# Even steps in a new order, and the keys' transpose moved to PSUM bank Y

## Chip, core and metric

The kernel runs on one core of one Trainium2 chip. The metric is the device time of one execution in microseconds (us). It is given as the median of several runs; a separate profiled execution has a time of its own, and its trace is where durations in this document come from.

## What is computed

An attention layer with 16 query heads and one shared pair of key and value heads, over 64 entries of 128 tokens with 512 features, in float32. For each entry:

```
xn  = layernorm(x, g_in)                       # 128 x 512
q   = xn @ Wq  -> 16 heads of 64, times 64**-0.5
k,v = xn @ Wkv -> 64 + 64, with one null key and value in front
sim = q k^T + attn_bias   (masked: causal, and the entry's padding)
out = softmax(sim) v      -> 128 x 1024
x   = x + layernorm(out @ Wo, g_out)
```

## The kernel before

The program is one long list of instructions whose order is written by hand: `manual_schedule()` keeps each engine's instructions in the order in which the Python code emits them. The tile framework adds semaphores wherever one instruction needs another's result or a buffer that another still uses. An engine works through its list in order, so an instruction that waits holds up all that stand behind it on its engine.

After a prologue, a loop calls `step(n)` for n = -6 to 62. One step works on several entries at once, each at another stage. Numbers below are for step n in the steady part of the loop:

- the queries of four entries (a group) are made over four steps, with seven products of half size in place of eight (`product(g, f, 1..7)`, line 436, names `pa`, `pc`, `pw`). Each product is four instructions on TensorE. Their results are read from PSUM by ScalarE (`keep`, names `ku`, `kp`, line 447; `q_out` without a name, line 454) or by VectorE (`q_out` with a name, line 457, `qT<-pc,ku` and `qT<-pw,kp`).
- the scores of entry n+2: `scores(b, 0)` and `scores(b, 1)` (line 500, `ps`) for lower and upper tokens. Both use the same PSUM buffer `s`, so the second half waits until VectorE has taken the first one out (`scores_add`, line 513). `scores_max` (line 518) finds the negated row maximum of each half.
- the softmax of entry n+1: `exps` on ScalarE (line 527, one instruction for each head row), `rinv` on VectorE (line 544), `scale` on GpSimd (line 548), `blocks_T` on VectorE (line 580, `sb`), and 14 DMAs (`blocks_move`, line 606) which put the transposed blocks into `aTb`.
- the values of entry n: `values` and `values_end` (line 641, `po`), taken out by ScalarE (line 685, `oT`). A one-element copy `done` (line 673) on VectorE stands between the two.
- keys and values of later entries: `k_T` (line 356) transposes the keys of entry n+5 and `kv_mm` (line 321) multiplies for entry n+6, both into one PSUM tile `pk`. VectorE reads `pk` three times: `kT_out` (line 361), and `kv_out` (lines 335 and 344).
- the output product, done for two entries together with seven products (`out_product`, line 755, names `pyX`, `pyY`, `pyw`, eight instructions each). Products 1, 2 and 4 stand in even steps, the others in odd steps. `out_part` (line 778) and `out_keep` (lines 767, 769) take results out.
- the output norm of the two entries of a pair, in even steps: `pair_stats`, `pair_pow` (GpSimd), `pair_nmr` (line 799, `nmro`, a tiny VectorE instruction), `pair_norm` (line 809, ScalarE writes `yn` into PSUM bank Y), `pair_residual` (VectorE: line 813 multiplies by `gob` in place in bank Y, line 814 adds the residual into `y`), then `store`.

All eight PSUM banks are in use: two for `s`, one each for `a`, `c`, `X`, `Y`, and two in turn for tag `w`. In the kernel before, `pk` is a `w` tile. Bank Y holds in turn `yn` of the first entry and `yn` of the second entry (even step), then `pyY` (odd step).

The instructions of a step that the prediction follows, in the order of the code for an even step: product 4 of the pair, first `exps`, `pair_stats`, `rinv(eb, 0)`, output product 1, query product 2, `pair_norm(p4)` and its residual, output product 2 (`pyw`), more `exps`, query product 1, the rest of `exps`, `rinv(eb, 1)`, `scale`, `pair_norm(p4 + 1)`, query product 5, `scores(nb, 0)`, `scores_add(nb, 0)`, `values`, `pair_residual(p4 + 1)`, `blocks_T`, `scores_max(nb, 0)`, `scores(nb, 1)`, `scores_add(nb, 1)`, `values_end`, query product 6, `k_T` and `kv_mm`, query product 7, `q_out(..., "c", "u3")`, `scores_max(nb, 1)`, `kT_out`, `kv_out`. In odd steps `scores_max(nb, 1)` comes ahead of product 6. The next step begins with query product 2 (odd steps), then query products 4 and 3; product 3 adds onto the bank `c` which `q_out(..., "c", "u3")` reads.

Of the kernel before, what the change touches and what calls it, by code (L numbers as in the profile page):

```python
# [8 lines left out]
FP = mybir.dt.float32  # L9
U8 = mybir.dt.uint8  # L10
AF = mybir.ActivationFunctionType
ALU = mybir.AluOpType
# [5 lines left out]
def kernel(  # L18
# [59 lines left out]
    nc = tc.nc  # L78
    B, N, DIM = x.shape
    H = attn_bias.shape[0]  # L80
    DH = w_kv.shape[1] // 2
    P = 128
# [3 lines left out]
    GB = 4  # L86
    NG = B // GB
    TOK = GB * N
    KVN = 2 * DH
# [22 lines left out]
    xs, res, m8s = {}, {}, {}  # L112
# [141 lines left out]
    def norm_stats(m):  # L254
        st = small.tile([P, 6], FP, tag="st", name=f"st_{m}")
        nc.vector.bn_stats(st, xs[m])
        mv = small.tile([P, 2], FP, tag="mv", name=f"mv_{m}")
        nc.vector.bn_aggr(mv, st)
        rstd = small.tile([P, 1], FP, tag="rstd", name=f"rstd_{m}")
        nc.vector.tensor_scalar(rstd, mv[:, 1:2], EPS, None, ALU.add)  # L260
        nc.gpsimd.tensor_tensor(rstd, rstd, nhalf, ALU.pow)  # L261
        stats[m] = mv, rstd
# [53 lines left out]
    def kv_mm(m, pkv=None):  # L316
        g, t = divmod(m, GB)
        if pkv is None:
            pkv = ps_w.tile([P, KVN], FP, tag="w", name=f"pkv_{m}")
        for kc in range(KC):  # L320
            nc.tensor.matmul(  # L321
                pkv,
                xT[g][:, t, kc, :],
                wkv[:, kc, :],
                start=(kc == 0),
                stop=(kc == KC - 1),
            )
        return pkv
# [3 lines left out]
    def kv_out(m, pkv):  # L332
        g, t = divmod(m, GB)
        k = bp.tile([P, 2, DH], FP, tag="ktok", name=f"ktok_{m}")
        nc.vector.tensor_tensor(
            k,
            pkv[:, 0:DH].unsqueeze(1).broadcast_to([P, 2, DH]),
            nkv[:, 0:DH].unsqueeze(1).broadcast_to([P, 2, DH]),
            ALU.subtract,
        )  # L340
        ktok[m] = k
        if t == 0:
            vs[g] = hp.tile([P, GB, DH], FP, tag="vs", name=f"vs_{g}", bufs=3)
        nc.vector.tensor_tensor(vs[g][:, t, :], pkv[:, DH:], nkv[:, DH:], ALU.subtract)
# [8 lines left out]
    def k_T(m, pk=None):  # L353
        if pk is None:
            pk = ps_w.tile([P, N], FP, tag="w", name=f"pkT_{m}")
        nc.tensor.transpose(pk, ktok.pop(m).rearrange("p r d -> p (r d)"), ident)
        return pk

    def kT_out(m, pk):
        kT[m] = hp.tile([P, N], FP, tag="kT", name=f"kT_{m}", bufs=6)  # L360
        nc.vector.tensor_copy(kT[m], pk)
# [83 lines left out]
    def keep(tag, name):  # L445
        kept[name] = bp.tile([P, HT], FP, tag=f"k{name}", name=f"k{name}", bufs=1)
        nc.scalar.copy(kept[name], prod[tag])  # L447
# [63 lines left out]
    def scores_add(b, hf):  # L511
        sv = S[b][:, :, KEYS[hf]].rearrange("p (r f) j -> p r f j", r=2)
        nc.vector.tensor_tensor(sv, pss.pop((b, hf)), sv, ALU.add)  # L513

    def scores_max(b, hf):
        if hf == 0:
            nmax[b] = small.tile([P, 2, R8], FP, tag="nmax", name=f"nmax_{b}")
        nc.vector.tensor_reduce(  # L518
            nmax[b][:, hf], S[b][:, :, WITH_NULL[hf]], AX.X, ALU.max, negate=True
        )  # L520

    def exps(b, hf, lo=0, hi=R8):
        if hf == 0 and lo == 0:
            rsum[b] = small.tile([P, 2, R8], FP, tag="rsum", name=f"rsum_{b}")
        for k in range(lo, hi):
            row = S[b][:, k, WITH_NULL[hf]]
            nc.scalar.activation(  # L527
                row,
                row,
                AF.Exp,  # L530
                bias=nmax[b][:, hf, k : k + 1],
                accum_out=rsum[b][:, hf, k : k + 1],
            )
# [8 lines left out]
    def rinv(b, hf):  # L542
        rinvs[b, hf] = small.tile([P, R8], FP, tag="rinv", name=f"rinv_{b}_{hf}")
        nc.vector.reciprocal(rinvs[b, hf], rsum[b][:, hf])
# [149 lines left out]
    def out_mm(b, lo=0, hi=NC):  # L694
        if lo == 0:
            pool, tag = ps_w, "w"
            if b > P_LAST:
                pool, tag = (ps_q, "c") if b == P_LAST + 2 else (ps_y, "XY"[b % 2])
            py = pool.tile([P, DIM], FP, tag=tag, name=f"py_{b}")
            ys[b] = py  # L700
        for c in range(lo, hi):
            nc.tensor.matmul(  # L702
                ys[b],
                oT[b][:, c, :],
                wo[:, c, :],
                start=(c == 0),
                stop=(c == NC - 1),
            )
# [14 lines left out]
    def plain(b):  # L723
        return not (paired(b) or paired(b - 1))
# [39 lines left out]
    def out_keep(tag, name, slot):  # L764
        kept[name] = bp.tile([P, HE], FP, tag=f"k{slot}", name=f"k{name}", bufs=1)
        if name == "yu2":
            nc.vector.tensor_copy(kept[name], prod["y" + tag])  # L767
        else:
            nc.scalar.copy(kept[name], prod["y" + tag])
# [26 lines left out]
    def pair_nmr(b):  # L796
        mv, rstd = yn.pop(b)
        nmr = small.tile([P, 1], FP, tag="nmro", name=f"nmro_{b}")
        nc.vector.tensor_scalar(nmr, mv[:, 0:1], rstd, -1.0, ALU.mult, ALU.mult)  # L799
        nmrs[b] = nmr, rstd  # L800
# [9 lines left out]

    def pair_residual(b):
        z = yn.pop(b)
        nc.vector.tensor_tensor(z, z, gob, ALU.mult)
        nc.vector.tensor_tensor(ys[b], z, res.pop(b), ALU.add)

    def out_stats(b):
        st = small.tile([P, 6], FP, tag="st", name=f"sto_{b}")
# [44 lines left out]
    def step(n):  # L862
        def ok(b, end=B):
            return 0 <= b < end
# [11 lines left out]
        p12, p4, p5673 = n - 1, n - 3, n - 2  # L876
        first, third, second = paired(p12), paired(p4), paired(p5673)
        one = ok(n - 1) and plain(n - 1)
        def transfers():

            if n == 1:
                store(0)
            if n > B3 + 1 and ok(n - 2) and plain(n - 2):
                store(n - 2)
            loads_late(n)

        fill = n <= 0
        eb = n + 1 if n < B3 else n + 2  # L890
# [17 lines left out]
                token_sum(qg, k)  # L908
        for m in mns:
            norm_stats(m)  # L910
        if n == -4:
            bias_add(0)
            bias_add(1)
# [42 lines left out]
        if n == B3 - 1:  # L956
            scores(B3 + 1, 1)
            scores_add(B3 + 1, 1)
            scores_max(B3 + 1, 1)
        if third:  # L960
            pair_stats(p4 + 1)
        if 2 * GB <= mb < B:
            tokens_T(mb)
            if (mb + 1) % GB == 0:
                tokens_out(mb // GB)
        if soft and n != 1:
            exps(eb, 0, 4)
        if fast and f == 0 and not fill:
            token_sum(qg, 1)
        if soft and n not in (1, B3 + 1):  # L970
            rinv(eb, 0)
            scale(eb, 0)
        if third:
            pair_pow(p4 + 1)
# [29 lines left out]
        if n == B3:  # L1004
            out_keep("X", "yp1", "p1")
            scores(eb, 0)
            scores_add(eb, 0)
            scores_max(eb, 0)
            out_product(p12, 2, ps_w, "w")
            pair_norm(p4)  # L1010
            pair_residual(p4)
            store(p4)
            out_part(p12, 0, "w", "yp1")
            scores(eb, 1)
            scores_add(eb, 1)
            exps_half(eb, 0)
            scores_max(eb, 1)
        elif first:
            out_keep("X", "yp1", "p1")
            out_product(p12, 2, ps_w, "w")  # L1020
            out_part(p12, 0, "w", "yp1")
        if soft and n != 1:
            exps(eb, 1, 2, 4)
        if soft and not second:
            exps(eb, 1, 4, 6)
        if fast:
            product(qg, f, 1, ps_q, "a")
            keep("a", "p1")
            q_out(qg, f, lo_t, "w", "p1")
# [20 lines left out]
        if fast and f == 0 and not fill:  # L1050
            for k in range(3, 5):
                token_sum(qg, k)
        if fast:
            product(qg, f, 5, ps_q, "c")
        if second:
            out_product(p5673, 7, ps_y, "X", start=False)
# [9 lines left out]
        if n == B3 - 1:  # L1066
            exps_half(B3 + 1, 0)
            exps(B3 + 1, 1, 0, 3)
        if sc and n != B3:
            scores(nb, 0)  # L1070
            scores_add(nb, 0)
        split = sc and n != B3
# [30 lines left out]
            scores_max(nb, 0)  # L1103

        late = fast and (first or n < 0)
        if sc:
            scores(nb, 1)
            scores_add(nb, 1)
            if n == -1:
                rinv(0, 1)  # L1110
                scale(0, 1)
            if not late:
                scores_max(nb, 1)
        if ok(n) and split:
            values_end(n, split)
            if n > B3 + 1:
                out_mm(n - 1, NF)
        if one and n > 1:
            out_stats(n - 1)
        if eb == B - 1:  # L1120
# [20 lines left out]
            scale(B3 + 1, 1)  # L1141
        if n + 10 < 2 * GB:
            norm_T(n + 10)
        if ok(mkv) and mkv >= GB - 1:

            pk = ps_w.tile([P, KVN + N], FP, tag="w", name=f"pk_{mkv}")
            k_T(mk, pk[:, KVN:])
            kv_mm(mkv, pk[:, 0:KVN])


        if (n + 8) % GB == 0 and 2 <= (n + 8) // GB < NG:
            tokens_in((n + 8) // GB)
# [7 lines left out]
                scores_max(nb, 1)  # L1160
        if second:
            pair_stats(p5673)
        if ok(mkv) and mkv >= GB - 1:
            kT_out(mk, pk[:, KVN:])
            kv_out(mkv, pk[:, 0:KVN])
        if ok(mk) and not ok(mkv):
            kT_out(mk, k_T(mk))
        if n == B3 - 2:
# [111 lines left out]
```

## Time and profile before

| what | value |
|---|---|
| median of 3 runs | 1109.07 us (1108.53 to 1110.0) |
| the profiled execution's own time | 1106.42 us |
| its span, first to last instruction | 1104.5 us |
| mean granted TensorE clock | 0.997 |
| busy: PE / PE weight loads | 1081.3 us / 868.1 us |
| busy: DVE (VectorE) / ACT (ScalarE) / POOL (GpSimd) | 795.7 / 665.5 / 706.0 us |
| idle of ACT before `oT` (line 685), waiting for PE | 198.0 us |
| idle of PE weight loads before `ps` (line 500), waiting for DVE line 513 | 25.6 us, 61 times |

How to read it: busy time is the union of an engine's instructions in the profiled execution. PE is the matrix multiplication and PEld the load of its weights, which overlaps it. Matmuls are pipelined and their ends are modelled, so small waits of TensorE are seen best in the weight loads, whose starts are recorded. "A <- B" says that A sat idle until B was done.

### The profile page before, as it was taken

To read this page: it belongs to the slowest core of one execution; us is meant where nothing else is said; L and a number is where in the kernel's file an instruction comes from. 1 tells how busy PE (TensorE), PEld (TensorE's weight loads), DVE (VectorE), ACT (ScalarE), POOL (GpSimd) and SP (SyncE) were. 2 spreads that over 40 slices of the span, in tenths; PEclk is the share of its full clock that TensorE was granted. 3 is DMA by queue.
4 is the path that set the end of the run, shared out by engine and by line. 5 is a ranking of instruction groups with operands and counts; after the bars stand their busy time and mean duration, and the time that the engine had idled before them with its cause. 6 is when DMAs were issued, how large, how long until landed. Compare 5 with 4: busy or idle time off the path is not lost.

```text
span 1104.5 us, 27326 instructions
## 1 busy us (share of the span) xinstructions
PE 1081.3 (98%) x9794; PEld 868.1 (79%) x9794; DVE 795.7 (72%) x1729; ACT 665.5 (60%) x2645; POOL 706.0 (64%) x521
## 2 busy tenths in 40 slices
PE   8999999999999999999999999999999999999987
PEld 5576788888888888888888888888888888888643
DVE  4676677877867877776886777787777787666852
ACT  3265567666666656566756566766666665657651
POOL 2546958566676756767575675856667675676832
PEclk9999999999999999999999999999999999999999
DMA  6422354453534444353353435445353453422333
GB/s 198 129 76 62 81 150 112 134 131 89 159 99 139 125 128 122 91 167 107 121 138 113 126 101 149 115 131 132 87 159 99 134 130 116 113 63 76 97 106 100
DMA packets 101062, 129.81 MB, mean 118 GB/s; under 512 B 21312, under 2 KB 65728, under 8 KB 99136
## 3 DMA queue, kind: packets, MB, share of 16 engines
q1 hardware_dynamic: 99680, 126.70, 41.0%
q8 instruction: 78, 1.28, 0.5%
q10 hardware_dynamic: 1248, 1.38, 0.4%
q14 instruction: 56, 0.46, 0.1%
HBM read 54.86 MB, written 31.46 MB: 78 GB/s over the span
## 4 chain that ended last, share of the span: by engine, by line
PE 81%; DVE 5%; DMA 4%; ACT 4%; SPq 3%; POOL 2%; issue 1%; DVEq 0%; POOLq 0%; ACTq 0%
PE pa L436 17%; PE pyX L755 16%; PE pc L436 8%; PE pyY L755 8%; PE ps L500 8%; PE po L641 7%; PE pk L321 4%; PE pw L436 4%; PE pyw L755 4%; DMA x<-in_x_dram 3%; PE py L702 3%; ACT s L527 2%; SPq L606 2%; PE pq L387 1%; DVE s L513 1%
## 5 line engine op out<-in xcount | busy, mean ns | idle before, releaser
L527 ACT ACTIVATE s<-s,nmax 128x65 f32<-128x65 f32 (+1 forms) x1024 | 371.5, 367 | 0.0
L479 POOL TENSOR_TENSOR s<-biasp,mneg 128x1552 f32<-128x1552 f32 x64 | 205.3, 3208 | 112.0 <-DVE sb L580 108.8
L548 POOL TENSOR_TENSOR s<-s,rinv 128x512 f32<-128x512 f32 (+1 forms) x128 | 189.6, 1482 | 122.6 <-DVE nmro L799 89.1
L685 ACT ACTIVATE oT<-po,nv 128x512 f32<-128x512 f32 x128 | 81.0, 683 | 198.0 <-PE po L641 198.0
L527 ACT ACTIVATION_READ_ACCUMULATOR s<-s,nmax 128x1 f32 x1024 | 194.7, 190 | 0.0
L755 PE MATMUL pyX<-wT,oT 128*128 128x256 f32 x696 | 164.7, 379 | 0.5 <-DVE kyu L767 0.5
L755 PEld LDWEIGHTS pyX<-wT,oT 128*128 128x128 f32 x696 | 131.8, 190 | 19.6 <-DVE kyu L767 0.9
L500 PEld LDWEIGHTS ps<-kT,qT 64*64 64x64 f32 x4096 | 92.5, 134 | 48.1 <-DVE s L513 25.6
L513 DVE TENSOR_TENSOR s<-ps,s 128x512 f32<-128x512 f32 (+1 forms) x128 | 121.6, 950 | 10.1 <-PE ps L500 9.6
L436 PE MATMUL pa<-xS,wq 128*128 128x256 f32 x480 | 123.6, 380 | 1.0 <-ACT ku L447 1.0
L518 DVE TENSOR_REDUCE nmax<-s 128x8 f32<-128x520 f32 (+1 forms) x128 | 120.1, 938 | 1.3
L500 PE MATMUL ps<-kT,qT 64*64 64x64 f32 (+1 forms) x4096 | 116.7, 251 | 3.7 <-DVE done L673 2.0
L580 DVE STREAM_TRANSPOSE sb<-s 128x1536 f32<-128x1536 f32 x62 | 109.9, 1773 | 11.6 <-POOL s L548 4.3
L641 PE MATMUL po<-aTb,vs 64*64 64x256 f32 (+1 forms) x1240 | 115.3, 379 | 0.0
L436 PEld LDWEIGHTS pa<-xS,wq 128*128 128x128 f32 x480 | 86.2, 190 | 11.2 <-ACT ku L447 1.8
L447 ACT COPY ku<-pa 128x256 f32<-128x256 f32 x120 | 44.7, 373 | 82.5 <-PE pa L436 82.5
L261 POOL TENSOR_TENSOR rstd<-rstd,nhalf 128x1 f32<-128x1 f32 x64 | 35.7, 558 | 60.4 <-DVE rstd L260 55.4
L436 PE MATMUL pa<-xS,wS 128*128 128x256 f32 x240 | 67.8, 405 | 0.1
L809 ACT ACTIVATE yn<-y,nmro,rstdo 128x512 f32<-128x512 f32 x58 | 45.4, 782 | 36.2 <-DVE nmro L799 36.1
L321 PE MATMUL pk<-wkv,xT 128*128 128x128 f32 x488 | 64.5, 275 | 0.0
L457 DVE TENSOR_TENSOR qT<-pw,kp 128x256 f32<-128x256 f32 x60 | 25.4, 424 | 53.4 <-ACT kp L447 53.4
L641 PEld LDWEIGHTS po<-aTb,vs 64*64 64x64 f32 (+1 forms) x1240 | 55.8, 134 | 9.7 <-issue 4.1
(116 smaller groups left out, 2068.9 us busy)
## 6 DMA issues: line engine op xcount, KB each, us to landing
aTb<-sb SPq DMA_DIRECT2D x369, 64.0 KB
x<-in_x_dram SPq DMA_DIRECT2D x64, 256.0 KB
res<-in_x_dram SPq DMA_DIRECT2D x64, 256.0 KB
out_dram<-y SPq DMA_DIRECT2D x64, 256.0 KB
aTb<-sb SPq DMA_DIRECT2D x492, 32.0 KB
xd<-xb SPq DMA_DIRECT2D x14, 1024.0 KB
xT<-xd SPq DMA_DIRECT2D x56, 256.0 KB
wo<-in_L_cond_Wo_dram SPq DMA_DIRECT2D x1, 2048.0 KB
```

The costliest lines, as they stand in the source:

```text
L321: nc.tensor.matmul(pkv, xT[g][:, t, kc, :], wkv[:, kc, :], start=(kc == 0), stop=(kc == KC - 1),)
L436: nc.tensor.matmul(prod[tag], w[:, kc, f * P : (f + 1) * P], t[:, :, kc, :], start=(start and kc == 0), stop=(kc == HK - 1), skip_group_ch ...
L479: nc.gpsimd.tensor_tensor(S[b], biasp, mneg[:, t].unsqueeze(1).broadcast_to([P, R8, ROW]), ALU.add,)
L500: nc.tensor.matmul(pv[u * DH : (u + 1) * DH, r, f, :], qT[g][rows, f, t, hf, u], kT[b][rows, 0:nk], start=True, stop=True,)
L513: nc.vector.tensor_tensor(sv, pss.pop((b, hf)), sv, ALU.add)
L518: nc.vector.tensor_reduce(nmax[b][:, hf], S[b][:, :, WITH_NULL[hf]], AX.X, ALU.max, negate=True)
L527: nc.scalar.activation(row, row, AF.Exp, bias=nmax[b][:, hf, k : k + 1], accum_out=rsum[b][:, hf, k : k + 1],)
L548: nc.gpsimd.tensor_tensor(sv, sv, rinvs.pop((b, hf)).unsqueeze(2).broadcast_to([P, R8, sv.shape[2]]), ALU.mult,)
L580: nc.vector.transpose(sb.rearrange("p j e q -> p e j q"), S[b][:, :, 1 : ROW - 1].rearrange("p e (j k) -> p e j k", k=Q),)
L641: nc.tensor.matmul(pos[b][u][r * DH : (r + 1) * DH, half], vals[keys], aT_of(b)[keys, slots, r * NF : (r + 1) * NF], start=start, stop=Tru ...
L685: nc.scalar.activation(oT[b][:, u * NF : (u + 1) * NF, :].rearrange("p f (s q) -> p s f q", q=Q), po[u].rearrange("p h i f q -> p (h i) f q"),
L755: nc.tensor.matmul(prod[key], h[:, c, :], w[:, c, :], start=(start and c == 0), stop=(c == HC - 1), skip_group_check=not start,)
```

## The change

No instruction is added or taken away. The order changes, one PSUM tile moves to another bank, and one operand changes place:

- In even steps with a full set of work (n = 4, 6, ..., 56; `even` in the code) `pair_nmr` of the pair's first entry moves from inside `pair_norm` to just behind `norm_stats`; `rinv(eb, 0)` comes ahead of `pair_stats`; query product 1 with its `keep` and `q_out` comes ahead of output product 2; and query product 5, `scores(nb, 0)` and `scores_add(nb, 0)` come ahead of the last `exps`, `rinv(eb, 1)`, `scale` and `pair_norm` of the pair's second entry.
- `k_T` comes straight behind `values_end`, ahead of query product 6; `kv_mm` keeps its place behind product 6. Their tile `pk` is now in bank Y (from step 0 on).
- From step 3 on (`early`), `kT_out` and `kv_out` come straight behind `kv_mm`: in odd steps ahead of `scores_max(nb, 1)`, in even steps ahead of query product 7 and `q_out(..., "c", "u3")`.
- `pair_residual` writes the product with `gob` to `ys[b]` in SBUF in place of bank Y, and adds the residual there.

```diff
     def pair_residual(b):
         z = yn.pop(b)
-        nc.vector.tensor_tensor(z, z, gob, ALU.mult)
-        nc.vector.tensor_tensor(ys[b], z, res.pop(b), ALU.add)
+        nc.vector.tensor_tensor(ys[b], z, gob, ALU.mult)
+        nc.vector.tensor_tensor(ys[b], ys[b], res.pop(b), ALU.add)
...
+        even = first and third and fast
...
+        pks = []
+        if ok(mkv) and mkv >= GB - 1:
+            pks.append(None)
+
+        def keys_T(pool, tag):
+            pks[0] = pool.tile([P, KVN + N], FP, tag=tag, name=f"pk_{mkv}")
+            k_T(mk, pks[0][:, KVN:])
+
+        def keys_values_out():
+            kT_out(mk, pks[0][:, KVN:])
+            kv_out(mkv, pks[0][:, 0:KVN])
...
         for m in mns:
             norm_stats(m)
+        if even:
+            pair_nmr(p4)
...
+        if even:
+            exps(eb, 0, 4)
+            rinv(eb, 0)
         if third:
             pair_stats(p4 + 1)
...
+        elif even:
+            out_keep("X", "yp1", "u3")
+            product(qg, f, 1, ps_q, "a")
+            exps(eb, 1, 2, 4)
+            keep("a", "p1")
+            q_out(qg, f, lo_t, "w", "p1")
+            out_product(p12, 2, ps_w, "w")
+            out_part(p12, 0, "w", "yp1")
+            exps(eb, 1, 4, 6)
+            product(qg, f, 5, ps_q, "c")
+            scores(nb, 0)
+            scores_add(nb, 0)
         elif first:
             out_keep("X", "yp1", "p1")
             out_product(p12, 2, ps_w, "w")
             out_part(p12, 0, "w", "yp1")
...
         late = fast and (first or n < 0)
+        early = fast and n > 2 and pks
         if sc:
             scores(nb, 1)
             scores_add(nb, 1)
...
-            if not late:
+            if not late and not early:
                 scores_max(nb, 1)
...
+        if pks and ok(n):
+            keys_T(ps_y, "Y")
...
-        if ok(mkv) and mkv >= GB - 1:
-
-            pk = ps_w.tile([P, KVN + N], FP, tag="w", name=f"pk_{mkv}")
-            k_T(mk, pk[:, KVN:])
-            kv_mm(mkv, pk[:, 0:KVN])
-
+        if pks:
+            if not ok(n):
+                keys_T(ps_w, "w")
+            kv_mm(mkv, pks[0][:, 0:KVN])
+            if early:
+                keys_values_out()
+                if sc and not late:
+                    scores_max(nb, 1)
...
-        if ok(mkv) and mkv >= GB - 1:
-            kT_out(mk, pk[:, KVN:])
-            kv_out(mkv, pk[:, 0:KVN])
+        if pks and not early:
+            keys_values_out()
```

At their old places the moved lines are skipped in even steps (`and not even`).

More of the change, by code (lines that the diff above doesn't have):

```diff
@@ L965, in step @@
                 tokens_out(mb // GB)
-        if soft and n != 1:
+        if soft and n != 1 and not even:
             exps(eb, 0, 4)
@@ L970, in step @@
         if soft and n not in (1, B3 + 1):
-            rinv(eb, 0)
+            if not even:
+                rinv(eb, 0)
             scale(eb, 0)
@@ L1021, in step @@
             out_part(p12, 0, "w", "yp1")
-        if soft and n != 1:
+        if soft and n != 1 and not even:
             exps(eb, 1, 2, 4)
-        if soft and not second:
+        if soft and not second and not even:
             exps(eb, 1, 4, 6)
-        if fast:
+        if fast and not even:
             product(qg, f, 1, ps_q, "a")
@@ L1052, in step @@
                 token_sum(qg, k)
-        if fast:
+        if fast and not even:
             product(qg, f, 5, ps_q, "c")
@@ L1068, in step @@
             exps(B3 + 1, 1, 0, 3)
-        if sc and n != B3:
+        if sc and n != B3 and not even:
             scores(nb, 0)
```

## The prediction

> **What bounds the kernel now.** I read the page first (busy times), then the list of waits, then the timelines of the weight loads and of DVE over neighbouring steps in the middle of the run.
>
> ```profile
> PE 1081.3 (98%) x9794; PEld 868.1 (79%) x9794; DVE 795.7 (72%) x1729; ACT 665.5 (60%) x2645; POOL 706.0 (64%) x521
> ```
>
> ```profile
> PEld ps L500 <- DVE s L513: 25.6, 61, 1.7
> ```
>
> TensorE is the bound: DVE, ACT and POOL have more than a quarter of the span to spare, and its one repeated wait is the second half of the scores, on the add that empties their PSUM buffer. So an edit is worth what it does to TensorE's waits. I number times from T0, the first weight load of `ps` in a step. Step 24 (even, T0 = 472.38), loads:
>
> ```profile
> 472.38 0.56 PEld L500 LDWEIGHTS ps<-kT,qT 64*64 64x64 f32 x32 [0.33 <-issue]
> ...
> 473.89 0.86 PEld L500 LDWEIGHTS ps<-kT,qT 64*64 64x64 f32 x32 [0.25 <-DVE s L513]
> ...
> 475.36 0.73 PEld L436 LDWEIGHTS pa<-xS,wS 128*128 128x128 f32 x4 [0.39 <-issue]
> 476.24 0.14 PEld L356 LDWEIGHTS pk<-ident,ktok 128*128 128x128 f32 x1
> ...
> 479.71 0.84 PEld L436 LDWEIGHTS pc<-xT,wS 128*128 128x128 f32 x4
> ...
> 489.51 0.56 PEld L500 LDWEIGHTS ps<-kT,qT 64*64 64x64 f32 x32 [0.33 <-issue]
> ```
>
> and the same step on DVE:
>
> ```profile
> 473.14 0.69 DVE L513 TENSOR_TENSOR s<-ps,s 128x512 f32<-128x512 f32 x1
> ...
> 474.21 0.69 DVE L813 TENSOR_TENSOR yn<-yn,gob 128x512 f32<-128x512 f32 x1
> ...
> 477.81 1.21 DVE L513 TENSOR_TENSOR s<-ps,s 128x1024 f32<-128x1024 f32 x1
> ...
> 478.94 0.41 DVE L457 TENSOR_TENSOR qT<-pc,ku 128x256 f32<-128x256 f32 x1
> ...
> 480.40 0.28 DVE L361 COPY kT<-pk 128x128 f32<-128x128 f32 x1
> ```
>
> The scores and values take 2.98 us (472.38 to 475.36), and the next step's scores begin at T0 + 17.13. Step 26 (T0 = 504.91) is disturbed:
>
> ```profile
> 502.38 0.78 ACT L809 ACTIVATE yn<-y,nmro,rstdo 128x512 f32<-128x512 f32 x1 [1.80 <-DVE nmro L799]
> ...
> 506.22 0.20 DVE L544 RECIPROCAL rinv<-rsum 128x8 f32<-128x8 f32 x1 [0.35 <-ACT s L527]
> ...
> 506.54 0.68 DVE L513 TENSOR_TENSOR s<-ps,s 128x512 f32<-128x512 f32 x1
> ...
> 507.28 0.86 PEld L500 LDWEIGHTS ps<-kT,qT 64*64 64x64 f32 x32 [0.68 <-DVE s L513]
> ```
>
> ACT waited for `nmro`, so the exponentials ended late, DVE stood at `rinv`, and the add behind it came at T0 + 1.63 in place of 0.76. Reading T0 to the next T0 in the same timelines, the even steps 6, 10, 14, ... 54 exceed 17.13 by 0.06, 0.14, 0.49, 0.21, 0.38, 0.86, 0, 0.69, 1.03, 0.16, 0.67, 0 and 0 us: 4.7 us in all. Steps 4, 8, 12, ... are at 17.13 every time. Those 4.7 us are all that a smoother even step can bring.
>
> **The change part by part.** The work is the same, so only waits move.
>
> *nmro early, rinv early, scores ahead of the last exponentials.* `nmro` gets behind `rstd` (500.07 in step 26) and `yn` follows 0.20 later, as at 502.19 and 502.38; it may start at about 500.6, when ACT's two exponentials of the upper half are through. That takes 1.8 us from ACT's delay, so the exponentials end about 0.5 us before T0, and the add stands ahead of `rinv`: it starts at T0 + 0.76 always. Gain 4.7 us. Query product 1 and `pyw` change places, four and eight instructions back to back on TensorE: nothing; `y<-pyw` then has until the second `po` tile, over 0.9 us.
>
> *The keys' wait.* `pk` now takes bank Y, so the transpose waits until DVE has multiplied the second entry's `yn` by `gob`. `nmro` of that entry now stands behind the add. From T0: add 0.76; `rinv` 0.60 later (506.54 to the next start, 507.14), `nmro` 0.12 later (506.22 to 506.34), `yn` on ACT 0.20 later, the multiply 0.81 after that (502.38 to 503.19), which takes 0.69, and a load starts 0.06 after DVE's end (473.83 to 473.89): 0.76 + 0.60 + 0.12 + 0.20 + 0.81 + 0.69 + 0.06 = 3.24. TensorE is there at 2.98. A wait of 0.26 in every even step; before, product 6 stood there and waited for nothing of the kind, and the multiply began at 1.83. Queued behind the transpose on TensorE is everything else. On DVE, the multiply stands idle for `yn`, and the residual, `blocks_T`, maximum and second add stand behind it.
>
> *The second wait.* From the multiply's start to the second add's start DVE needs 3.60 (474.21 to 477.81), so the add starts at 2.49 + 3.60 = 6.09. Then `qT<-pc,ku` used to follow 1.13 later; now the three reads of `pk` stand between, 0.20 + 0.19 + 0.14 = 0.53 (480.40, 480.60, 480.79, 480.93). So it starts at 6.09 + 1.13 + 0.53 = 7.75, ends 0.41 later, and releases bank `c` at 8.22. The reader of that release is query product 3 of the next step, which adds onto bank `c`: TensorE is there at 479.71, T0 + 7.33, and with the first wait at 7.59. Before, `qT` ended at T0 + 6.97 and left 0.36 to spare. Now 8.22 - 7.59 = 0.63 more is waited. The rest of DVE's delay goes into idle time of the odd step (it waits 1.85 us for `pyX` at 521.28). In odd steps the same three reads delay `qT` from 6.72 to about 7.1, its end to 7.5, and product 3 stands there at 8.19: hidden by an output product between.
>
> [...]
>
> *Residual in SBUF.* The multiply reads PSUM and writes SBUF, as line 814 does (0.69 against 0.70). The add now has both operands in SBUF; the nearest row is line 399, 128x1024 in 1.21, so about 0.61 in place of 0.69. Bound: 0 to 0.08 off the second wait, at most 2.2 us; I take 0.
>
> *DMAs.* No queue's order changes. `blocks_T` in even steps comes 0.67 later (multiply at 2.49 for 1.83), so 14 DMAs of `aTb` do, but TensorE's next values come 0.89 later as well. No charge; if TensorE did not wait, that cover would be gone. In the start, step 2 still reads `pk` late (its `vs` ends near T0 + 9.3, `pyY` stands at 9.06), and `pyY` now shares the bank: 0.3 once.
>
> Sum: 26 even steps (4 to 54) x 0.89 = 23.1; step 56 has scores of a later entry ahead of product 3 (it stands at 8.15), so 0.26 alone; 0.3 at the start; less 4.7: **+19.0 us**. Against the profiled execution's 1106.42 that is 1125.4. The median of the runs is 1109.07, 2.65 above it, so I predict 1128.1.
>
> **The rivals.**
>
> *Faster: the two waits do not come.* They need the second entry's `yn` early: if the multiply ended by T0 + 2.92 in place of 3.18 and `qT` by 7.27 in place of 8.16, only the 4.7 us would show: 1109.07 - 4.7 = 1104.4. So it turns at 0.26 us for the first wait and 0.89 for the second, in one chain through DVE and ACT; where both waits together come to 0.17 in each of 27 steps, gain and loss are equal. For it: the exponentials end before T0, so ACT is free; only `nmro`'s place behind the add holds `yn`. Against it: DVE works in order, and every term is a recorded duration.
>
> *The keys' wait alone.* If DVE makes up its 0.9 us before `qT`, 27 x 0.26 = 7.0, less 4.7, plus 0.3: 1111.7. For it there is little: between the multiply and `qT` no row of step 24 shows idle time.
>
> *Slower still: late blocks.* If `aTb`'s DMAs land late, the values wait too. In step 25 `sb` waited 0.60 until 491.92 for a transfer of the step before, just when the last values loads stood there (491.83), so there is little slack in that step. A further 0.4 in each of 27 pairs gives +11: 1139. Against it: TensorE's own delay of 0.89 is larger than that of the blocks.
>
> **How the numbers follow.** Both waits: 0.76. Faster: 0.10. Keys' wait alone: 0.08, of which I count half as within 0.2% (2.2 us, about what a measurement of this kernel can tell from no change). Slower still: 0.06. So faster 0.10, same 0.04, slower 0.86. For the range, each of the two waits may be off by 0.1 through a term or the bounds above, 0.2 x 27 = 5.4 us; with the skirts of the smaller and larger case I give 1118 to 1135.
>
> **What would show it.** In the profile after: `pk` L356 loads at T0 + 3.2 with about 0.26 more idle before them, released by DVE line 813's new place; `pc<-xT,wS` in steps after even ones idle about 0.6, released by `qT` L457, at T0 + 8.2; even steps 18.0 long, all alike; odd steps 15.4 as before; ACT's wait before `yn` of the first entry gone. The prediction is wrong if `pk` or `pc` shows no wait in even steps, if even steps fall to 17.13, or if the loads of `po` begin to wait for DMAs.

## The result and the profile after

The changed kernel takes 1127.97 us (median of 4 runs, 1126.79 to 1128.2). Four runs of the kernel before gave 1108.8 (1107.4 to 1110.0). The ratio is 1.0174, with a 95% interval of 1.0158 to 1.019. The profiled execution of the changed kernel took 1127.95 us, with a span of 1126.1 us and a granted clock of 0.997, as before. The median rose by 19.2 us; from profile to profile (1106.42 to 1127.95) the rise is 21.5 us.

First the busy times on the page of the kernel after. TensorE is busy for 96% of the span, where it was 98%; DVE and POOL have gained 3.9 and 11.2 us of busy time with the same instructions:

```profile
PE 1086.3 (96%) x9794; PEld 869.2 (77%) x9794; DVE 799.6 (71%) x1729; ACT 661.9 (59%) x2645; POOL 717.2 (64%) x521
```

Then the waits of the weight loads after (idle us in total, times, longest). Two that the list of before did not have, or hardly had, now stand near the top:

```profile
PEld ps L500 <- DVE s L513: 23.7, 59, 1.3
PEld pc L436 <- DVE qT L457: 21.8, 28, 1.2
...
PEld pk L356 <- DVE y L813: 18.0, 27, 0.7
```

Step 24 of the kernel after shows both (T0 = 479.19). Weight loads:

```profile
479.19 0.56 PEld L500 LDWEIGHTS ps<-kT,qT 64*64 64x64 f32 x32 [0.33 <-issue]
...
482.48 0.14 PEld L356 LDWEIGHTS pk<-ident,ktok 128*128 128x128 f32 x1 [0.70 <-DVE y L813]
482.49 0.79 PEld L436 LDWEIGHTS pa<-xS,wS 128*128 128x128 f32 x4
...
487.58 0.73 PEld L436 LDWEIGHTS pc<-xT,wS 128*128 128x128 f32 x4 [0.83 <-DVE qT L457]
...
497.28 0.56 PEld L500 LDWEIGHTS ps<-kT,qT 64*64 64x64 f32 x32 [0.33 <-issue]
```

DVE in the same step:

```profile
479.95 0.69 DVE L513 TENSOR_TENSOR s<-ps,s 128x512 f32<-128x512 f32 x1 [1.09 <-PE ps L500]
...
480.67 0.16 DVE L799 TENSOR_SCALAR nmro<-mvo,rstdo 128x1 f32<-128x1 f32 x1
...
481.74 0.69 DVE L813 TENSOR_TENSOR y<-yn,gob 128x512 f32<-128x512 f32 x1 [0.61 <-ACT yn L809]
482.46 0.82 DVE L814 TENSOR_TENSOR y<-y,res 128x512 f32<-128x512 f32 x1
...
485.47 1.20 DVE L513 TENSOR_TENSOR s<-ps,s 128x1024 f32<-128x1024 f32 x1
...
487.13 0.40 DVE L457 TENSOR_TENSOR qT<-pc,ku 128x256 f32<-128x256 f32 x1
```

The transpose into `pk` loads at T0 + 3.29, right behind the multiply by `gob`; product 3 loads at T0 + 8.39, right behind `qT<-pc,ku`; the next step begins at T0 + 18.09. Of the 0.70 idle ahead of the transpose 0.39 is old: step 24 of the kernel before has it as "issue" ahead of product 6, which stood there. All even steps from 4 to 54 take 18.09 to 18.15 except step 34 (19.32), and in all of them the first add stands at T0 + 0.76 to 0.82. The odd steps take 15.35 or 15.42, in turn.

A measure that serves for all kernels below is the pair, two steps, from the first load of `pyw` to the first load of the next `pyw`. Before, pairs take 32.53 and, in turn with it, 32.60 to 33.63 (the late even steps); after, 33.45 and 33.52, with one of 34.75. The first pair and the last stand outside these figures.

### The profile page after: what moved, and what is told of

The parts are those of the page before. It is cut to its first block, busy times and chain, and to the rows that moved or that the text cites. A ratio compares the mean times of both kernels' runs of the same rounds, so it can differ in the third digit from the quotient of the medians.

```text
span 1126.1 us, 27325 instructions
## 1 busy us (share of the span) xinstructions
PE 1086.3 (96%) x9794; PEld 869.2 (77%) x9794; DVE 799.6 (71%) x1729; ACT 661.9 (59%) x2645; POOL 717.2 (64%) x521
## 4 chain that ended last, share of the span: by engine, by line
PE 62%; DVE 15%; DMA 9%; SPq 5%; ACT 4%; issue 3%; POOL 1%; DVEq 0%; ACTq 0%; POOLq 0%
PE pyX L755 15%; PE pa L436 11%; PE pyY L755 8%; PE pc L436 7%; PE ps L500 5%; DVE sb L580 4%; DMA x<-in_x_dram 4%; DVE s L513 4%; SPq L606 4%; PE po L641 3%; DMA out_dram<-y 3%; PE pyw L755 3%; PE py L702 3%; PE pk L321 2%; ACT s L527 2%
## 5 line engine op out<-in xcount | busy, mean ns | idle before, releaser
L755 PEld LDWEIGHTS pyX<-wT,oT 128*128 128x128 f32 x696 | 131.9, 190 | 20.4 <-POOL oT L737 1.2
L436 PE MATMUL pc<-xT,wS 128*128 128x256 f32 x240 | 64.4, 391 | 10.1 <-DVE qT L457 10.1
L321 PEld LDWEIGHTS pk<-wkv,xT 128*128 128x128 f32 x488 | 63.9, 192 | 3.0
```

Source lines behind the costliest of these rows:

```text
L321: nc.tensor.matmul(pkv, xT[g][:, t, kc, :], wkv[:, kc, :], start=(kc == 0), stop=(kc == KC - 1),)
L436: nc.tensor.matmul(prod[tag], w[:, kc, f * P : (f + 1) * P], t[:, :, kc, :], start=(start and kc == 0), stop=(kc == HK - 1), skip_group_ch ...
L755: nc.tensor.matmul(prod[key], h[:, c, :], w[:, c, :], start=(start and c == 0), stop=(c == HC - 1), skip_group_check=not start,)
```

## Experiments

The change has three parts: the order of the even steps (O), bank Y with the early reads (B), and the residual in SBUF (R). The first runs take one part out, the next do one part alone, and the last ones move one instruction or two more. The first four ran on one chip, the others on another. The kernel before, run beside them, took 1107.91 us on either chip, and 1108.94 us beside the last three runs.

**O and R, without B.**

```diff
-        early = fast and n > 2 and pks
+        early = False
...
-        if pks and ok(n):
-            keys_T(ps_y, "Y")
...
-            if not ok(n):
-                keys_T(ps_w, "w")
+            keys_T(ps_w, "w")
```

> Edit: the changed kernel without its bank move. pk is a tile of tag w again, transposed behind product 6, and read by DVE at the end of the step; the new order of even steps and the residual in SBUF stay. Theory (one chain: add of the first scores, nmro, yn, multiply, residual, blocks_T, second add, three reads of pk, qT, bank c): the wait before pk goes, and the three reads (0.53 us) leave the chain, so qT ends near T0 + 7.83 and product 3 waits about 0.56 us of the 1.07 us that both waits took together. Even steps 17.6 to 17.7 us, median about 1118.5 us. Rival 1 (the whole loss is the transpose's wait for bank Y): no wait is left, about 1104 us. Rival 2 (the loss comes from blocks_T and its DMAs being late): they are as late as in the changed kernel, about 1128 us.

Measured: 1119.66 us (1117.41 to 1122.72), ratio 1.0106 (1.008 to 1.0131); most pairs 33.03, near the expected 1118.5. The new order and R cost 11.8 us with the keys where they were, so bank Y is not the whole loss. The multiply stands at T0 + 2.55 here too, and `qT` ends at 7.82, past the 7.33 at which product 3 was ready.

**B and R, in the old order.**

```diff
-        even = first and third and fast
+        even = False
```

> Edit: the changed kernel with the old order of even steps (even = False); pk in bank Y, transposed straight behind the last values and read early, residual in SBUF. Theory: nmro stands ahead of the add again, the multiply starts at T0 + 1.83 and ends before the transpose's turn at 2.97, so pk does not wait; qT stands 0.53 us later behind the reads, ends near 7.55, and product 3 (7.33) waits 0.2 to 0.4 us. The late steps n = 6, 10, ... keep their 4.7 us. Median 1113 to 1117 us. Rival 1 (transpose's wait alone): no loss, about 1108 us. Rival 2 (late blocks): blocks_T is as early as before, about 1108 us.

Measured: 1122.28 us (1119.81 to 1126.21), ratio 1.013 (1.01 to 1.016), more than expected. Steps 4, 8, 12, ... take 17.24, but steps 10, 14, ... 54 take 18.0 to 19.2, with the first add as late as T0 + 2.77. (Step 6 takes 20.95; the granted clock over it is 0.92, where it is 1.00 in most of the run.) None of the theories had that; the run with R alone below finds it.

**O and B, with the old residual.**

```diff
-        nc.vector.tensor_tensor(ys[b], z, gob, ALU.mult)
-        nc.vector.tensor_tensor(ys[b], ys[b], res.pop(b), ALU.add)
+        nc.vector.tensor_tensor(z, z, gob, ALU.mult)
+        nc.vector.tensor_tensor(ys[b], z, res.pop(b), ALU.add)
```

> Edit: the changed kernel with the old residual: multiply in place in bank Y, then the add from bank Y. Bank Y then comes free one DVE instruction later, at about T0 + 4.03 in place of 3.30, so the transpose waits about 1.05 us in place of 0.32. Theory: only the end of the chain counts. The add does not read two SBUF operands any more, so the chain ends at about 8.28; TensorE comes to product 3 at 7.33 + 1.05 = 8.38. The second wait vanishes and the time stays: even steps 18.1 us, median 1126 to 1129 us. Rival 1 (the transpose's wait is the loss): 27 x 0.73 = 20 us more, about 1148 us.

Measured: 1127.93 us (1126.58 to 1128.54), ratio 1.0177 (1.0162 to 1.0192); pairs 33.49 and 33.56. The waits of this kernel:

```profile
PEld pk L356 <- DVE y L814: 36.8, 27, 1.4
...
PEld pc L436 <- DVE qT L457: 2.0, 2, 1.1
```

The wait at the transpose has doubled, since bank Y is now free only after the add, and the wait at product 3 is gone. In step 24 the multiply starts at T0 + 2.55 as in the kernel after, the transpose loads at 4.03, `qT` ends at 8.22, and product 3 loads at 8.33 without a wait, 0.06 from where it stood in the kernel after. So the time is the same: the chain that begins with the late multiply reaches TensorE at two places, about 1.0 us late at each, and TensorE pays once. (That the two places are equally late is chance.)

**The three reads behind `qT` in even steps.**

```diff
-            if early:
+            if early and not late:
                 keys_values_out()
...
             q_out(qg, HC + f, hi_t, "c", "u3")
+            if early and late:
+                keys_values_out()
```

> Edit: in even steps the three reads of pk stand behind qT<-pc,ku and ahead of the upper maximum, in place of ahead of qT; all else as in the changed kernel. Theory: the transpose's wait stays at 0.32 us, qT comes 0.53 us earlier and ends near 7.83, product 3 (ready at 7.65) waits 0.24 us in place of 0.75. Even steps 17.6 us, 26 x 0.51 = 13.3 us less: about 1114.7 us. Rival 1 (transpose's wait) and rival 2 (late blocks): nothing changes, 1128 us.

Measured: 1120.65 us (1118.13 to 1122.13), ratio 1.0111 (1.0091 to 1.013); pairs 32.99 for 33.45. The direction is as expected and the size is not: 7.3 us of the 13.3. `qT` still starts at T0 + 7.42, because the second add stands at 6.29 and not at the 6.09 that I had worked with, so about 0.30 of idle stays at product 3, and most pairs shorten by 0.46. From profile to profile, steps 4 to 55 shorten by 10.5 us in all, for two steps of 18.80 (30 and 34) have late values and a long residual add, as step 34 of the kernel after. The start takes 3.6 us of that back (the first `pyw` at 110.2 for 106.7), and there the clock differs: it is 0.83 from 10 to 20 us and again from 40 to 50, where the kernel after has 1.00. By an estimate from these figures, 2 x 10 x 0.17 = 3.4 us, that part of the shortfall may come with the granted clock and not with the edit.

**R alone.** The kernel before, with the residual of the changed kernel.

```diff
-        nc.vector.tensor_tensor(z, z, gob, ALU.mult)
-        nc.vector.tensor_tensor(ys[b], z, res.pop(b), ALU.add)
+        nc.vector.tensor_tensor(ys[b], z, gob, ALU.mult)
+        nc.vector.tensor_tensor(ys[b], ys[b], res.pop(b), ALU.add)
```

> The kernel before, with one edit: the multiply by the output gain writes its result to SBUF, and the residual add has both operands in SBUF. Order and banks are the old ones. Theory: such an add, but not the old one with an operand in PSUM, stands still while GpSimd works in SBUF (0.82 to 1.72 us in the trace of after where it was 0.69 in all 58 places before). In the old order the first entry's add of steps 6, 10, 14, ... lies beside the shift of the query group on GpSimd, and behind it on VectorE stand the output partials, then the exponentials and the scores: 0.7 to 1.0 us in each of 13 steps, so 1117 to 1121. Rival: the add's place is worth at most its own shortening (the prediction's 0 to 0.08 us each): 1107 to 1108, no change.

Measured: 1125.84 us (1122.23 to 1128.99), ratio 1.0169 (1.0146 to 1.0192), above the expected 1117 to 1121. Two lines of code in the old order cost nearly as much as the whole change. Step 26 of the kernel before, DVE and POOL:

```profile
503.93 0.69 DVE L814 TENSOR_TENSOR y<-yn,res 128x512 f32<-128x512 f32 x1
504.54 0.41 DVE L778 TENSOR_TENSOR y<-pyw,kyp 128x256 f32<-128x256 f32 x1
```

```profile
503.87 1.27 POOL L418 TENSOR_TENSOR xS<-xT,xS 128x512 f32<-128x512 f32 x1
```

The same place with R alone, DVE, POOL and ACT:

```profile
509.09 1.77 DVE L814 TENSOR_TENSOR y<-y,res 128x512 f32<-128x512 f32 x1
510.78 0.41 DVE L778 TENSOR_TENSOR y<-pyw,kyp 128x256 f32<-128x256 f32 x1
```

```profile
509.04 1.27 POOL L418 TENSOR_TENSOR xS<-xT,xS 128x512 f32<-128x512 f32 x1
```

```profile
511.28 0.37 ACT L447 COPY kp<-pa 128x256 f32<-128x256 f32 x1 [1.10 <-DVE y L778]
```

In both, the add begins 0.05 or 0.06 after the shift of the query group on GpSimd has begun. With an operand in PSUM it takes 0.69. With both in SBUF it ends 0.55 after GpSimd's end (509.04 + 1.27 = 510.31, and 510.86): 1.08 us longer. `y<-pyw` behind it is late by that, ACT waits 1.10 for it, the exponentials end late, and the first add of the next scores with them. Of the pairs, 32.53 stay as they were and the others rise from 32.60 to 33.63 to as much as 34.29 (one 36.40). The size per step was right: in this trace steps 6, 10, 14, ... without step 34 are 0.89 longer on the average than before, for the 0.7 to 1.0 of the theory. What the sum lacked lies elsewhere. Step 34 takes 20.93 (the pair of 36.40), with a granted clock of 0.92 over it for the 1.00 over step 38, and step 57, close to the end, takes 20.02 for 17.81, with 0.91. This profiled execution took 1122.23 us, the least of the four; of the others, up to 1128.99, there is no trace. All four have a mean clock of 0.991 to 0.993, the kernel before beside them 0.996 to 0.998. An estimate from these figures, 0.004 x 1120, is that 4 to 5 us of the 17.9 may come with the clock; why it was lower is not shown.

**O alone.** Both edits of the runs without B and with the old residual.

> The new order alone: keys back in bank w with their late reads, and the old residual with the product in PSUM. Theory: the second add returns from T0 + 6.28 (new order with the residual in SBUF) to 6.09, so the even steps shorten from 17.57 to about 17.38, and the disturbed steps of that run go: 1112 to 1115. What is left over the kernel before is nmro behind the first add, which keeps the multiply at 2.5. Rival 1 (the SBUF add costs nothing in this order): 1119.7 again. Rival 2 (without the bank the new order is a plain gain of 4.7): 1103.

Measured: 1114.27 us (1113.65 to 1116.13), ratio 1.0058 (1.0044 to 1.0072); most pairs 32.91. The time is as expected: the second add comes at T0 + 6.16 for the 6.29 with R, most even steps take 17.45, and 5.4 us go that the run of O and R had. The disturbed steps do not go: 6, 30, 38 and 42 take 18.0 to 18.3, with the copy `done` late. What else stays is `nmro` behind the first add.

**The changed kernel with `yn` ahead.**

```diff
             product(qg, f, 5, ps_q, "c")
+            exps(eb, 1, 6)
+            rinv(eb, 1)
+            scale(eb, 1)
+            pair_norm(p4 + 1)
             scores(nb, 0)
             scores_add(nb, 0)
...
-        if soft and not second:
+        if soft and not second and not even:
             exps(eb, 1, 6)
...
-        if third and n != B3:
+        if third and n != B3 and not even:
             pair_norm(p4 + 1)
```

> The kernel after with one move: in even steps the last exponentials, rinv, the scale, nmro and yn of the second entry stand ahead of the scores and their add, in place of behind. Bank Y, the early reads and the residual in SBUF stay. Theory: yn is through on ScalarE at T0 + 0.8, the multiply follows the first add at T0 + 1.44 in place of 2.55, the transpose to bank Y finds it free at 2.2 (TensorE comes at 2.98), and the qT end at 7.1 is ahead of product 3 (7.33); so in steps 4, 8, 12, ... both waits vanish (step 17.0). In steps 6, 10, 14, ... the residual add at 2.13 meets GpSimd's shift of the query group (1.9 to 3.1) and is held about 1 us, which brings up to 0.75 us of the second wait back. 1098 to 1108. Rival 1 (bank Y or the early reads cost by themselves, wherever the multiply stands): 1117 or more. Rival 2 (rinv ahead of the add makes the add late again): even steps 6, 10, ... irregular with the add past T0 + 0.8.

Measured: 1118.45 us (1115.05 to 1121.19), ratio 1.0091 (1.0068 to 1.0114): a miss, 10 us above the range. The multiply went from 2.55 to 1.83 only, not to 1.44, and steps 4, 8, 12, ... keep a wait of 0.29 at product 3 (17.24 in place of 17.0). In steps 6, 10, 14, ... the residual add is longer beside GpSimd, as expected (in step 30 it takes 1.29, to 0.56 past the end of GpSimd's operation), and every other pair takes 32.97 to 34.21. And 6.7 of the 13.9 us by which its span is above that of before lie in steps 56 and 57: in step 56 the add takes 2.94, to 0.54 past the end of a GpSimd operation of 3.23, the second half of the scores waits 2.55 for the adds, and the granted clock over the two steps is 0.95 and 0.84.

**The same with the old residual.**

> As the run before, and the residual as it was (product in PSUM, so bank Y is free only after the add). Theory: the multiply at T0 + 1.44 and the add behind it end at 2.9, just ahead of the transpose at 2.98, and the add is not held by GpSimd: no wait in either kind of even step, all of them about 17.0, odd steps 15.38: about 1097 (1095 to 1100), faster than both kernels. Rival 1 (the bank's wait returns because the transpose now stands behind the add): 0.3 to 0.7 in each of 27 steps, 1105 to 1116. Rival 2 (bank Y or the early reads cost by themselves): 1117 or more.

Measured: 1110.23 us (1107.76 to 1112.88), ratio 1.0018 (1.0008 to 1.0027). Rival 1 came true, with a wait of 0.32 (17.41) in most even steps: the add ends at 3.24 and not at 2.9. Step 24 (T0 = 472.46) says why, DVE and the transpose:

```profile
473.83 0.20 DVE L273 TENSOR_SCALAR nmr<-mv,rstd 128x1 f32<-128x1 f32 x1
474.22 0.16 DVE L673 COPY done<-po 128x1 f32<-128x1 f32 x1 [0.18 <-PE po L641]
474.29 0.69 DVE L813 TENSOR_TENSOR yn<-yn,gob 128x512 f32<-128x512 f32 x1
475.02 0.69 DVE L814 TENSOR_TENSOR y<-yn,res 128x512 f32<-128x512 f32 x1
```

```profile
475.76 0.14 PEld L356 LDWEIGHTS pk<-ident,ktok 128*128 128x128 f32 x1 [0.71 <-DVE y L814]
```

With `yn` early, the multiply waits for nothing of its own: in DVE's order it stands behind the one-element copy `done`, which waits for TensorE's values. That copy was hidden in both traces that I had read, because there the multiply came late or had slack.

**The multiply ahead of `done`.** On top of the last run:

```diff
+    def pair_gain(b):
+        nc.vector.tensor_tensor(yn[b], yn[b], gob, ALU.mult)
...
+        if even and n != B3:
+            pair_gain(p4 + 1)
         if ok(n):
             values(n, split)
```

`pair_residual` then leaves the multiply of that entry out. In this kernel the multiply is line 814 and the add line 821.

> As the run with yn ahead and the old residual, and one move more: in even steps the multiply of the second entry stands ahead of the copy done<-po on VectorE. In that run the copy waited for the values until T0 + 1.76 and held the multiply at 1.83, so the add ended at 3.24 and the transpose waited 0.32 (0.71 idle). Theory: the multiply now starts at 1.45 to 1.6, the add ends at 2.9 to 3.05, the transpose waits 0 to 0.1 (idle 0.39 to 0.5), the second add comes at 5.1 and the qT end at 7.2: even steps of about 17.0 all alike, odd ones 15.38. 1096 to 1100, faster than both kernels. Rival 1 (the copy, now later by the multiply, holds the last values loads at T0 + 2.33 instead): even steps 17.2 to 17.5, 1104 to 1111. Rival 2 (bank Y costs wherever the multiply stands): 1110 again.

Measured: **1100.28 us** (1099.87 to 1102.76), ratio 0.9931 (0.9916 to 0.9947), 8.7 us below the kernel before, and just above the expected 1096 to 1100. Step 24 of this kernel (T0 = 469.80), DVE and weight loads:

```profile
471.29 0.69 DVE L814 TENSOR_TENSOR yn<-yn,gob 128x512 f32<-128x512 f32 x1
471.89 0.15 DVE L673 COPY done<-po 128x1 f32<-128x1 f32 x1
472.01 0.69 DVE L821 TENSOR_TENSOR y<-yn,res 128x512 f32<-128x512 f32 x1
```

```profile
469.80 0.56 PEld L500 LDWEIGHTS ps<-kT,qT 64*64 64x64 f32 x32 [0.33 <-issue]
...
472.77 0.14 PEld L356 LDWEIGHTS pk<-ident,ktok 128*128 128x128 f32 x1 [0.39 <-DVE y L821]
...
477.08 0.84 PEld L436 LDWEIGHTS pc<-xT,wS 128*128 128x128 f32 x4
...
486.88 0.56 PEld L500 LDWEIGHTS ps<-kT,qT 64*64 64x64 f32 x32 [0.33 <-issue]
```

The transpose is at T0 + 2.97, where TensorE arrived in the kernel before, product 3 stands without a wait, and the step takes 17.08 for the 17.13 of before, as most even steps do (step 6 takes 17.53, step 46 17.37). Pairs are 32.43 and mostly 32.50 to 32.60.

**`yn` ahead, the keys back in bank w, the old residual.** The first of these edits with those of the run of O alone.

> The new order with yn, nmro and rinv of the second entry ahead of the scores; keys back in bank w with late reads, and the old residual. Theory: the multiply is at T0 + 1.83 as in the kernel before, the qT end at 6.97 ahead of product 3 (7.33), no add is late any more: all even steps at 17.13, odd ones at 15.43. The 4.7 us of the late steps are gained: 1102 to 1105. Rival (the order costs something by itself, for which nmro's place was not the cause): 1108 to 1114.

Measured: 1104.32 us (1102.8 to 1105.4), ratio 0.9959 (0.9945 to 0.9973). The order is no loss once `yn` is early, as expected, and the multiply is back at 1.83. But the theory has more than came: steps 4, 8, 12, ... take 17.13, and of the others eight take 17.37 to 17.94, so that in the profiled executions steps 4 to 55 gain 0.8 us in place of 4.7. The median fell within the range all the same. In those eight steps the first add is on time and the copy `done` is late, because its values came late. The trace shows what held them: the last of the 14 `blocks_move` DMAs is issued at T0 - 0.8 in step 42 and at T0 - 1.1 in steps 6 and 30, where step 4 has T0 - 3.1. In these three steps the issues stood 1.5 to 1.8 us on SyncE until a load of `x` from HBM had landed (line 606 waiting for the DMA `x<-in_x_dram`). The late steps of the run of O alone have the same wait (1.8 to 2.7 us in steps 6, 30 and 38).

**B alone,** the old order and the old residual.

> Bank Y and the early reads alone, in the old order, with the old residual in PSUM. Theory: even steps 4, 8, 12, ... as in the run with yn ahead and the old residual (17.41, a wait of 0.32 at the transpose), steps 6, 10, 14, ... with the late add of the kernel before on top (0.4 on the average, 4.7 in all): 1111 to 1115, and so 8 to 11 us below the bank run with the residual in SBUF (1122.3). Rival (the SBUF add was not what made that run long): 1119 or more.

Measured: 1111.27 us (1108.43 to 1112.8), ratio 1.0024 (1.0012 to 1.0037), 11 us below the run of B and R. As expected: steps 4, 8, 12, ... take 17.41 and the transpose stands at 3.30.

The parts side by side, as the difference from the kernel before that ran with each, in us:

| | old residual | residual in SBUF (R) |
|---|---|---|
| old order, bank w | 0 | +17.9 |
| O | +6.4 | +11.8 |
| B | +2.3 | +14.4 |
| O and B | +20.0 | +19.2 (the change) |

The parts don't add. O and B cost 6.4 and 2.3 alone and 20.0 together, for O makes the multiply late and B makes TensorE wait for it. R costs most alone (4 to 5 us of it perhaps by the clock, as estimated above), and nothing on top of O and B: it frees bank Y 0.7 earlier and makes the chain to `qT` longer, and in the changed kernel the second entry's add is 0.13 longer in nearly every even step, where with R alone the first entry's was up to 1.1 longer.

## Why the prediction was right, step by step

- **The gain of 4.7 us** came: the first add is on time in every even step. One of the thirteen steps read for it was of another kind: in step 14 of the kernel before the first add stands at T0 + 0.77, and `done` at 2.27 for 1.76, so its 0.49 came from late values. Step 34 alone is 1.2 us longer after, where `done` waited for the values and the residual add took 1.57.
- **The first wait**, 0.26 by the sum: the transpose is at 3.29 for 3.24 and TensorE was there at 2.98, so 0.31. The multiply starts at 2.55 for 2.49. Each link of the chain (add, `rinv`, `nmro`, `yn`, multiply) is in the trace in that order, and the runs with `rinv`, `nmro` and `yn` ahead show that their place behind the add made it late.
- **The second wait**, 0.63 by the sum: product 3 loads at 8.39 for 8.22, and TensorE was there at 7.33 + 0.31, so about 0.75. The three reads ahead of `qT` are in it as computed, and moving them took 0.46 off the pair.
- **The residual in SBUF was the mis-sized term.** I took 0, with a bound of 0.08 to the good. In step 24 the add took 0.82 for 0.69, and the second add came at 6.28 for 6.09: 0.06 of that from the multiply, 0.13 from here. GpSimd works beside this add too: its `scale` ends at 482.74, and the add at 483.28, 0.54 later.

```profile
480.83 1.91 POOL L548 TENSOR_TENSOR s<-s,rinv 128x1024 f32<-128x1024 f32 x1 [4.86 <-DVE nmro L799]
```

  The sign was wrong, and the nearest row misled: an add of the same kind on another line told its length, not what GpSimd does beside it. The error was small only in this order; R alone went with +17.9 us.
- **Odd steps** were to stay as they were; they became 0.05 shorter. The start: step 2 takes 18.32 for 18.00, so the 0.3 that I charged is there. **Step 56**, for which the sum had 0.26, is 0.76 longer: the scores that stand ahead of product 3 there wait 0.83 for the second add, where they waited 0.33. **Step 57**, which the sum did not have, is 1.3 us longer: its residual adds take 1.72 and 1.70 for 0.69. The step takes 17.8 to 18.0 in all the kernels with the old residual and 19.0 or more in all those with R.
- **The sum**, from profile to profile: 26 even steps x (18.10 - 17.13) = 25.2, less 4.7, plus 1.2 for step 34, less 26 x 0.05 = 1.3 in the odd steps, is 20.4; steps 56 and 57 add 2.1, the rest of the end adds 0.2, and step 4 begins 1.2 us earlier than before, where the kernel before had a granted clock of 0.83 from 10 to 20 us and the kernel after 1.00. That gives the 21.5 by which the profiles differ. I had 19.0. The predicted median of 1128.1 still met 1127.97, because the 2.65 by which the median of before lay above its profile is not there after: its median and its profile agree to 0.02. Why is not shown; fewer late steps may be the reason. So two errors of 2.5 us each cancelled there, which is luck; the range of 1118 to 1135 did not need it.
- **The rivals.** *Late blocks* came in one steady step, 34. There the values begin again at T0 + 1.81, after 1.15 of idle:

```profile
648.38 0.17 PEld L641 LDWEIGHTS po<-aTb,nv 64*64 64x64 f32 x2 [1.15 <-DVE nmr L273]
```

  The `nmr` that it names is no operand of `po`. The last block DMA is issued at T0 - 0.42, where step 32 has T0 - 3.09, after the issues had stood 1.6 us until a load of `x` had landed. The kernel before has such waits as well (line 606 for `x`, 9.6 us in 11 waits; after, 6.9 us in 9), so they are not new with the change; here the late values made the multiply late (3.04), and the residual add behind it met GpSimd. Loads of `po` that wait for DMAs were one of the prediction's signs of being wrong; it came in this one step and cost 1.2 us. *The keys' wait* did not come alone. *The faster rival* named the right conditions, a multiply that ends by T0 + 2.92 and a `qT` that ends by 7.27. The change meets neither. With `yn` ahead and the residual in SBUF only the first is met (2.51, and 7.49), and a wait at product 3 stays. The kernel that meets both (`qT` at 7.15, multiply at 2.18 and the add, which frees its bank Y, at 2.90) is the fast one.
- **TensorE's loads.** The idle 0.70 and 0.83 ahead of 482.48 and 487.58 hold no weight load; product 6's stands behind the transpose, at 482.49. So in step 24 no load of a later product filled either wait.

## What to carry to other kernels

When a buffer is moved to a bank that another chain frees, follow that chain to its first late link on every engine, one-element copies included, and move that link first: here the same order, bank and residual gave +20.0 us with the multiply at T0 + 2.55 and -8.7 us with it at 1.49. Two waits that hung on one chain through DVE were not paid twice here: with the first wait three times as long (1.05 for 0.31) the second was gone and the time the same. An operand moved from PSUM to SBUF was not free: the add that had taken 0.69 us took up to 1.78 beside GpSimd, in the same order and banks. And a difference of a few us is compared with the granted clock of both runs before it is put down to an edit.

## What the runs showed of the hardware

The longer adds beside GpSimd were unexpected. Over all 58 residual adds (min/median/max in ns, then the first and last start), of the kernel before, the kernel after and R alone:

```profile
L814 DVE TENSOR_TENSOR y<-yn,res x58: 690/691/693, 143.4 to 1057.7; 128x512 f32<-128x512 f32 x58
```

```profile
L814 DVE TENSOR_TENSOR y<-y,res x58: 691/814/1724, 141.6 to 1079.0; 128x512 f32<-128x512 f32 x58
```

```profile
L814 DVE TENSOR_TENSOR y<-y,res x58: 691/720/1778, 144.0 to 1074.3; 128x512 f32<-128x512 f32 x58
```

With one operand in PSUM the add took 690 to 693 ns in these 58 places, also beside GpSimd (step 26 above); with both in SBUF it took 691 to 1724 ns in the kernel after and 691 to 1778 with R alone. In the kernel after, the adds of 0.81 us or more, 31 of the 58, all ended 0.54 or 0.55 us after a GpSimd operation that had begun before them; in step 26 of R alone it was 0.55, in steps 30 and 56 with `yn` ahead 0.56 and 0.54. GpSimd's next operation was longer too: in step 34 of the kernel after, the add took 1.57 and ended at 651.89, and the GpSimd operation that had begun at 651.30 took 1.74 us, where the same operation in the same step had taken 1.27 (the first of the two lines):

```profile
646.61 1.27 POOL L418 TENSOR_TENSOR xS<-xT,xS 128x512 f32<-128x512 f32 x1
651.30 1.74 POOL L418 TENSOR_TENSOR xS<-xT,xS 128x512 f32<-128x512 f32 x1
```

The numbers above agree with an operation that waits for the end of the other and is not merely slowed: the add took from 0.81 to 2.94 us in these places, and its end stayed 0.54 to 0.56 us behind GpSimd's. What would make it wait is not shown.
